# y in the side work's PSUM bank: a fixed window for C h, a third bank for A dt

## The chip, the cores and the metric

The kernel runs on one core of one Trainium2 chip. The metric is the device time of one execution in microseconds; before the change it was 2876.79 us (median of three runs, 2875.39 to 2877.91). All times below are microseconds unless marked otherwise. TensorE multiplies matrices into PSUM, which has eight banks of 512 float32 values for each of 128 partitions; VectorE (DVE), ScalarE (ACT) and GpSimd (POOL) do the elementwise work, and the sync engine's queue (SP) issues the DMAs.

## The reference, cut to what matters

The input x is 2 sequences of 1024 tokens with 512 features. The first block is a selective state space model whose state has 512 x 128 values a token; the second is a gated feed-forward net. Both are followed by a layer norm.

```python
xn = rms_norm(x) * norm_w
xn = xn * sigmoid((xn @ select_proj_w.T + select_proj_b) * select_gate)
delta, B_ssm, C_ssm = split(xn @ x_proj_w.T)            # 128 columns each
dt = softplus(delta @ dt_proj_w.T + dt_proj_b)
A = -exp(A_log)
# for every token, in order:
h = exp(dt[:, :, None] * A) * h + (dt * xt)[:, :, None] * bt[:, None, :]
y = einsum('bdn,bn->bd', h, ct)
# then
x = layernorm(x + (y + x * D_param) @ out_proj_w.T)
x = layernorm(x + (silu(x @ w_gate.T) * (x @ w_up.T)) @ w_down.T)
```

## The kernel before

**Steps, halves, groups.** The 2048 tokens are cut into 64 steps of 32 tokens (S). A step is worked in two halves of 256 features each, and a half in eight groups of 32 features; `k` counts the 1024 groups, `h` the 128 halves, and `r = k % 8` is the group's place in its half. One group's state history, 32 features by 32 tokens for all 128 state values (partitions), is one scan of 1024 elements on VectorE (L708).

**What a group does.** TensorE forms `bu`, the term (dt x) B, with two matmuls (L692) from `du`, a diagonal layout that GpSimd builds (L385), and A dt for the *next* group with two matmuls (`decay_mm`, L404) from `ddt` (L375). ScalarE takes the exponential of each A dt bank (`decay_exp`, L411) into one of three `a_sb` buffers. VectorE adds the carried state to the first token of `bu` (L705; not in the first step of a sequence) and runs the scan. The bu and a matmuls of one group use different rows of the array and run beside each other.

**PSUM.** `ps_bu` has two tiles of two banks each, `ps_a` two banks, `ps_m` one bank (the tag "m" of `misc`), `ps_y` one bank. The bank of `misc` is shared by all side work of the loop: one side group fills it, another engine evacuates it, then the next may fill it.

**C h.** y is formed from the finished state history of a half while the next half runs: `y_round(h, b)` is four matmuls of 32 columns of output partitions each (L423), for eight values of b. `ROUNDS` says in which groups of the next half these rounds are issued: three in r = 1, three in r = 4, two in r = 7. y of both halves of a step lies in one bank, and `y_out` (L430) brings it out once a step: a ScalarE copy (L436) and three GpSimd operations (L437 to L439). After four steps `post` is queued.

**Side work.** Everything else is written as generators that a `Work` object steps: `pre` (projections for the next lot of tokens: ss, sel, xp, b, z, uT, t0), `post` (transposes zT, output projection op, first layer norm), `ffn` (transpose x1T, gate and up products gu, down products d, second norm) and `silu`. A generator yields "E" for work on other engines, "P" ahead of a group of TensorE work that needs the bank, and "H" between the parts of a group. `others` steps each "E" item once in each group of the main loop; `tensor` runs one part. A side group holds the bank from its first part until `others` has issued its evacuation in a later group, so at most one side group can end, and one begin, between two calls of `others`. `PARTS` gives the parts that each r earns; unused credit is kept up to 6, and at most 4 parts are run in a group. A gate/up group has 8 parts of two matmuls, a half of a down product 8 parts of one, op 8, sel and xp 4, the transposes and z 2.

**Order.** Each engine runs its instructions in the order of issue. In a group the order of issue is: `others`; at r = 0 the half's start (y_out of the step before in a step's second half; in its first half a new `pre`, `work.finish` if the next step needs a lot that isn't ready, and `load` of the next step); the bu and a matmuls; the exponentials with L705 between them; the scan; the y rounds; the side parts; then one diagonal layout of GpSimd and at certain r the carry of the state (`carry_h`, `carry_a`). `carry_a` (L348) multiplies on GpSimd and takes an exponential on ScalarE at r = 5 of a step's first half. What is left of post and ffn when the loop ends runs after it, with six banks.

Of the kernel before, what the change touches and what calls it, by code (L numbers as in the profile page):

```python
# [9 lines left out]
FP = mybir.dt.float32  # L10
AF = mybir.ActivationFunctionType
# [6 lines left out]
TC = 256  # L18


ROUNDS = ((), (0, 1, 2), (), (), (3, 4, 5), (), (), (6, 7))
PARTS = (4, 0, 3, 3, 0, 3, 3, 0)
RMS_EPS = 1e-6
LN_EPS = 1e-5

# [9 lines left out]
def kernel(  # L35
# [83 lines left out]
    pre_pool = tc.alloc_tile_pool(name="pre", bufs=1)  # L119
    step_pool = tc.alloc_tile_pool(name="step", bufs=2)  # L120
    half_pool = tc.alloc_tile_pool(name="half", bufs=2)
    ps_y = tc.alloc_tile_pool(name="ps_y", bufs=1, space=PSUM)
    ps_m = tc.alloc_tile_pool(name="ps_m", bufs=1, space=PSUM)

    bank_pool = [tc.alloc_tile_pool(name="ps_m0", bufs=6, space=PSUM)]
# [39 lines left out]
    def pre(c):  # L165
# [31 lines left out]
        yield "E"  # L197
        for m in range(NM):
            nc.scalar.activation(xT[:, m, :], xT[:, m, :], AF.Copy, scale=col(V_NORM, m))
        yield "P"  # L200
        ps = misc(f"ss_{c}")
        for k in range(NM):
            nc.tensor.matmul(  # L203
# [9 lines left out]
        for a in (slice(0, 2), slice(2, 4)):  # L213
# [1 line left out]
                xn[:, a, :], xT[:, a, :], rms.unsqueeze(1).to_broadcast([P, 2, n]), ALU.mult  # L215
            )
            yield "E"
        yield "P"


        for m in range(NM):
            ps = misc(f"sel_{c}_{m}")
            yield from matmuls(ps, sel_w, m, xn)
            nc.scalar.activation(
                u[:, m, :], ps[:, 0:n], AF.Relu,
                bias=neg[:, 1, m : m + 1], scale=neg[:, 0, m : m + 1],
            )
            nc.scalar.activation(
                dt[:, m, :], ps[:, 0:n], AF.Abs, bias=gate_b[:, m : m + 1], scale=col(V_GATE, m)
            )  # L230
            yield "P" if m + 1 < NM else "E"
        yield from softplus(dt, u)
        nc.scalar.activation(dt, dt, AF.Exp, scale=-1.0)
        yield "E"
        for a in (slice(0, 2), slice(2, 4)):
            nc.gpsimd.tensor_tensor(xn[:, a, :], xn[:, a, :], dt[:, a, :], ALU.mult)
            yield "E"
        yield "P"


        for g, dst in ((0, low), (2, c_sb)):
            ps = misc(f"xp_{c}_{g}")
            yield from matmuls(ps, xp_w, g, xn)
            nc.scalar.copy(dst, ps[:, 0:n])
            yield "P"

        ps = misc(f"b_{c}")
        for j in range(n_j):
# [8 lines left out]
        for st in range(n_s):  # L257
# [2 lines left out]
                ub_d[t0 // S + st, :, :, 1, :].rearrange("g t n -> t g n"),  # L260
                rows.unsqueeze(1).to_broadcast([S, 4, N]),
            )
        yield "P"

        for a in range(0, NM, 2):
            ps = misc(f"z_{c}_{a}")
            for m in (a, a + 1):
                nc.tensor.matmul(  # L268
                    ps[:, ts(m - a, n)], dt_w[:, ts(m, P)], low, start=True, stop=True
                )  # L270
                yield "H" if m == a else "E"
            for m in (a, a + 1):
                z = ps[:, ts(m - a, n)]
                nc.scalar.activation(u[:, m, :], z, AF.Relu, bias=col(V_DTB, m))
                nc.scalar.activation(dt[:, m, :], z, AF.Abs, bias=col(V_DTB, m))
            yield "P" if a == 0 else "E"
        yield from softplus(dt, u)
        for a in (slice(0, 2), slice(2, 4)):
            nc.gpsimd.tensor_tensor(u[:, a, :], dt[:, a, :], xn[:, a, :], ALU.mult)
            yield "E"  # L280

        for j in range(n_j):
            yield "P"
            ps = misc(f"uT_{c}_{j}")
            for m in range(NM):
                nc.tensor.transpose(ps[:, ts(m, P)], u[:, m, ts(j, P)], ident)
                if m == 1:
                    yield "H"
            yield "E"
            t = pre_pool.tile([P, D], FP, tag="row", name=f"uT_{c}_{j}")  # L290
            nc.scalar.copy(
                t.rearrange("p (g m c) -> p m g c", g=4, m=NM),
                ps.rearrange("p (m g c) -> p m g c", m=NM, g=4),
            )
            for st in range(4):
                nc.sync.dma_start(
                    ub_d[t0 // S + 4 * j + st, :, :, 0, :].rearrange("g t q -> t g q"),
                    t[ts(st, S), :].rearrange("t (g q) -> t g q", g=4),
                )
            if c == 0:  # L300
                load(0)
                diag(0, 0)
                diag(0, 1)
        yield "P"
        ps = misc(f"t0_{c}")
        for m in range(NM):
            nc.tensor.matmul(
# [40 lines left out]
    def carry_a(st):  # L348

        if st % NSB == 0:  # L350
            return
        cd = carried[st]
        nc.gpsimd.tensor_tensor(cd, a_n, cd, ALU.mult)
        nc.scalar.activation(cd, cd, AF.Exp, scale=-1.0)

    def carry_h(st, i):

# [57 lines left out]
    def y_round(h, b):  # L415


        st, i = divmod(h, 2)
        if i == 0 and b == 0:
            ys[st] = ps_y.tile([P, 512], FP, tag="y", name=f"y_{st}")  # L420
        at = 28 + 28 * b
        for m in range(NM):
            nc.tensor.matmul(  # L423
                ys[st][ts(m, 32), ts(i, 256)], cz[st % 3][:, at : at + 32],
                hs[h][:, ts(m, 64), ts(b, 4)],
                start=(i == 0 and b == 0), stop=(i == 1 and b == 7),
                skip_group_check=True,
            )

    def y_out(st):  # L430

        tt, s = divmod(st, 4)
        if s == 0:
            yrs[tt] = post_pool.tile([P, 4, P], FP, tag="yr", name=f"yr_{tt}")
        yc = post_pool.tile([P, P, 4], FP, tag="yc", name=f"yc_{st}")
        nc.scalar.copy(yc, ys.pop(st).rearrange("p (q t) -> p q t", t=4))  # L436
        nc.gpsimd.tensor_tensor(yc, yc, pick.unsqueeze(1).to_broadcast([P, P, 4]), ALU.mult)  # L437
        nc.gpsimd.tensor_tensor(yc[:, :, 0:2], yc[:, :, 0:2], yc[:, :, 2:4], ALU.add)
        nc.gpsimd.tensor_tensor(yrs[tt][:, s, :], yc[:, :, 0], yc[:, :, 1], ALU.add)  # L439
        if s == 3:  # L440
            work.add(post(tt), front=True)

    yrs = {}
# [1 line left out]
    def post(tt):  # L445
# [4 lines left out]
        yield "E"  # L450
        nc.gpsimd.tensor_tensor(zT, zT, dq.unsqueeze(2).to_broadcast([P, NM, P]), ALU.mult)
        yield "E"
        yield "P"
        ps = misc(f"zT_{tt}")
        for s in range(4):
            nc.tensor.transpose(ps[:, ts(s, P)], yrs[tt][:, s, :], ident)
# [6 lines left out]
        )  # L463
        x1 = post_pool.tile([P, D], FP, tag="x1", name=f"x1_{tt}", bufs=4)
        nc.sync.dma_start(x1, xf[tt])
        yield "P"
        ps = misc(f"op_{tt}")
        for half in (slice(0, 256), slice(256, 512)):
            for k in range(NM):
# [20 lines left out]
    def ffn(tt, row):  # L490
# [22 lines left out]
            yield "E"  # L513
        fetch(4)
        x1T = ffn_pool.tile([P, NM, P], FP, tag="x1T", name=f"x1T_{tt}")
        yield "P"
        ps = misc(f"x1T_{tt}")
        for m in range(NM):
            nc.tensor.transpose(ps[:, ts(m, P)], row[:, ts(m, P)], ident)
# [5 lines left out]
        for what in order:  # L525
            part = int(what[1])
            if what[0] == "g":
# [2 lines left out]

                for f in range(0, NH, 2):
                    fetch(at + 4)
                    yield "P"
                    ps = misc(f"gu_{tt}_{part}_{f}")
                    for b in range(2):
                        w = pieces[at + b].rearrange("p (a k h) -> p a k h", a=2, k=NM)
# [17 lines left out]
                yield "E"  # L554
            for half in range(2):
                fetch(at + 4)
                yield "P"
# [49 lines left out]
    class Work:  # L607


        def __init__(self):  # L610
            self.gens, self.holder = [], None

        def add(self, gen, front=False):
            item = [gen, next(gen)]
# [13 lines left out]
                        self.holder = None  # L628
                    self.step(item)

        def tensor(self):

            if self.holder is not None:
                if self.holder[1] != "H":
                    return False
                self.step(self.holder)
                return True
            for item in self.gens:
                if item[1] == "P":
                    self.holder = item  # L640
                    self.step(item)
                    return True
            return False

        def finish(self, item):
            while item in self.gens:
# [13 lines left out]
    bank_pool.pop().release()  # L660
    bank_pool.append(ps_m)
    ps_bu = tc.alloc_tile_pool(name="ps_bu", bufs=2, space=PSUM)
    ps_a = tc.alloc_tile_pool(name="ps_a", bufs=2, space=PSUM)
    for b in range(2):
        decay_exp(0, b, decay_mm(0, b))

    pres, begun, credit = {}, set(), 0
    for k in range(NG):
        h, m, pair = place(k)
        st, i = divmod(h, 2)  # L670
        r = k % 8
        work.others()
        if r == 0:
            hs[h] = half_pool.tile([P, 256, S], FP, tag="h", name=f"h_{h}")

            if i == 1 and st:
                y_out(st - 1)
            if i == 0:
                c = lot_of[st]
# [31 lines left out]
            bu.rearrange("p q t -> p (q t)"),  # L711
            0.0, ALU.mult, ALU.add,
        )
        if h:
            for b in ROUNDS[r]:
                y_round(h - 1, b)
        credit = min(credit + PARTS[r], 6)
        for _ in range(min(credit, 4) if PARTS[r] else 0):
            if not work.tensor():
                break  # L720
            credit -= 1

        j, r4 = divmod(k, 4)
        if r4 == 3:
# [7 lines left out]
                carry_h(st + 1, 0)  # L732
        if r == 5 and i == 0 and st + 1 < NS:
            carry_a(st + 1)
    for j in range(8):
        y_round(2 * NS - 1, j)
    y_out(NS - 1)
    ps_a.release()
    ps_bu.release()
    bank_pool[0] = tc.alloc_tile_pool(name="ps_m2", bufs=6, space=PSUM)  # L740
# [4 lines left out]
        work.others()  # L745
        work.tensor()

    for pool in (bank_pool[0], ps_m, ps_y, hid_pool[0], ffn_pool, post_pool, main):
        pool.release()


# [65 lines left out]
```

## Time and profile before

| | |
|---|---|
| median of 3 runs | 2876.79 |
| profiled execution, its own time | 2875.05 |
| its span | 2873.2 |
| granted TensorE clock, mean | 0.985 |
| first scan starts, last scan ends | 42.5, 2785.2 |
| DVE scan L708 | 1024 x 2.287 |
| DVE carry add L705 | 992 x 0.187 |
| ACT exponential L411 | 2048 x 0.585 busy 1089.0 |
| GpSimd diagonals L375, L385 | 512 x 1.048 and 512 x 1.049 |
| ACT copy of y L436 | 64 x 0.585 |
| GpSimd L437, L438, L439 | 64 x 1.039, 0.612, 0.415 |
| ScalarE waiting for A dt (L411 on L404) | 957.1 in 710 waits |
| TensorE weight loads of a waiting for ACT | 19.9 in 68 waits |
| GpSimd ddt waiting for a's matmuls | 310.2 in 100 waits |

A float32 matmul appears as two records. Busy times of one engine are unions, so matmuls that run beside each other count once. In a row of a group the last part is the idle time of the engine just before such instructions and what ended most of it. In rows in order of time the first number is the start from the span's beginning, the second the length, and a bracket gives idle time before the row and what ended it.

### The profile page before, as it was taken

The numbers are of one execution on the slowest core, as the hardware profiler recorded it, in microseconds if no ns is written. First come the engines' busy times: TensorE is split into PE (matmuls) and PEld (weight loads), VectorE is DVE, ScalarE is ACT, GpSimd is POOL, SyncE is SP. The second block draws the span as 40 slices with busy tenths as digits, with TensorE's granted clock in tenths as the row PEclk, the third lists the DMA queues.
The fourth block names the chain that finished last, engine by engine and source line by source line (L and its number), as shares of the span: only waits on it lengthen the run. The fifth ranks groups of instructions, "written<-read, shape, count | busy, mean of one in ns | idle before, by whom it ended". The sixth has DMA issues, their size and how long they took to land.

```text
span 2873.2 us, 57382 instructions
## 1 busy us (share of the span) xinstructions
PE 2751.4 (96%) x22728; PEld 1496.3 (52%) x22728; DVE 2532.2 (88%) x2176; ACT 1561.8 (54%) x3105; POOL 1783.0 (62%) x2016
## 2 busy tenths in 40 slices
PE   7879899999999999999999999999999999999998
PEld 4324455555555555455555555555555555555558
DVE  3999799899998999999999999999999999999970
ACT  4545555555565556645555555555556555555543
POOL 4556665666666666666567667566665666666643
PEclk6999999999999999999999999999999999999999
DMA  2011221324213231222312233122321322333236
GB/s 74 16 30 65 78 87 61 105 66 133 85 53 112 89 107 62 82 98 89 111 51 88 97 103 109 56 84 92 114 96 51 115 96 91 114 101 100 98 112 230
DMA packets 112379, 258.66 MB, mean 90 GB/s; under 512 B 11568, under 2 KB 49456, under 8 KB 112112
## 3 DMA queue, kind: packets, MB, share of 16 engines
q1 hardware_dynamic: 112112, 254.99, 27.4%
q8 instruction: 181, 2.97, 0.4%
q14 instruction: 86, 0.70, 0.1%
HBM read 242.23 MB, written 12.71 MB: 89 GB/s over the span
## 4 chain that ended last, share of the span: by engine, by line
PE 75%; DVE 18%; issue 3%; ACT 2%; POOL 1%; DMA 0%; SPq 0%; DVEq 0%; POOLq 0%; ACTq 0%
PE bu L692 27%; PE gu L539 17%; DVE h L708 16%; PE y L423 13%; PE d L561 6%; PE a L404 5%; PE sel L186 2%; PE op L470 1%; PE xp L186 1%; DVE bu L705 1%; ACT a_sb L411 1%; PE b L250 1%; PE ss L203 0%; PE z L268 0%; DMA ub_d<-uT 0%
## 5 line engine op out<-in xcount | busy, mean ns | idle before, releaser
L708 DVE TENSOR_TENSOR_SCAN h<-a_sb,bu 128x1024 f32<-128x1024 f32 x1024 | 2341.2, 2287 | 160.7 <-PE bu L692 46.3
L411 ACT ACTIVATE a_sb<-a 128x496 f32<-128x496 f32 x2048 | 1089.0, 585 | 1078.5 <-PE a L404 957.1
L404 PE MATMUL a<-ddt,a_t 32*128 32x512 f32 x4096 | 1253.9, 647 | 3.0 <-ACT t L314 2.8
L692 PE MATMUL bu<-du,ub 32*128 32x512 f32 x4096 | 1210.5, 647 | 47.9 <-DVE h L708 27.3
L375 POOL TENSOR_TENSOR ddt<-dt,hot 128x512 f32<-128x512 f32 x512 | 532.6, 1048 | 310.2 <-PE a L404 310.2
L539 PEld LDWEIGHTS gu<-x1T,w 128*128 128x128 f32 x4096 | 482.2, 192 | 230.9 <-issue 181.3
L385 POOL TENSOR_TENSOR du<-ub,hot 128x512 f32<-128x512 f32 x512 | 535.0, 1049 | 48.9 <-PE a L404 44.9
L539 PE MATMUL gu<-x1T,w 128*128 128x128 f32 x4096 | 537.1, 283 | 11.7 <-DVE x L474 4.0
L692 PEld LDWEIGHTS bu<-du,ub 32*128 32x128 f32 x4096 | 342.9, 185 | 376.9 <-issue 206.8
L423 PE MATMUL y<-h,cz 128*32 128x256 f32 x8192 | 527.3, 386 | 1.3 <-DVE h L708 1.3
L423 PEld LDWEIGHTS y<-h,cz 128*32 128x32 f32 x8192 | 228.2, 110 | 407.8 <-issue 296.4
L404 PEld LDWEIGHTS a<-ddt,a_t 32*128 32x128 f32 x4096 | 379.4, 185 | 31.3 <-ACT a_sb L411 19.9
L579 POOL TENSOR_SCALAR gu<-gu 128x256 f32<-128x256 f32 x128 | 108.3, 846 | 309.6 <-ACT gu L547 309.3
L705 DVE TENSOR_TENSOR bu<-bu,cd 128x32 f32<-128x32 f32 x992 | 185.6, 187 | 98.2 <-PE a L404 92.0
L561 PE MATMUL d<-w,hid 128*128 128x256 f32 x1024 | 256.7, 393 | 12.6 <-ACT t L314 4.4
L561 PEld LDWEIGHTS d<-w,hid 128*128 128x128 f32 x1024 | 183.9, 190 | 131.7 <-issue 86.1
L437 POOL TENSOR_TENSOR yc<-yc,pick 128x512 f32<-128x512 f32 x64 | 66.5, 1039 | 151.1 <-ACT yc L436 151.0
L362 POOL TENSOR_TENSOR cd<-cd,h 128x256 f32<-128x256 f32 x124 | 106.4, 858 | 45.5 <-DVE h L708 45.5
L587 POOL TENSOR_TENSOR hid<-gu,e 128x256 f32<-128x256 f32 x128 | 93.0, 727 | 62.1 <-ACT e L585 60.2
L547 ACT COPY gu<-gu 128x512 f32<-128x512 f32 x128 | 75.1, 587 | 63.2 <-PE gu L539 63.1
L580 POOL TENSOR_TENSOR gu<-gu 128x256 f32<-128x256 f32 x128 | 94.2, 736 | 10.7
L567 DVE TENSOR_TENSOR x<-x,d 128x256 f32<-128x256 f32 x64 | 25.6, 399 | 72.3 <-PE d L561 72.3
(86 smaller groups left out, 1272.1 us busy)
## 6 DMA issues: line engine op xcount, KB each, us to landing
w<-in_wgu_s_dram SPq DMA_DIRECT2D x256, 512.0 KB, 3.6
w<-in_wd_s_dram SPq DMA_DIRECT2D x128, 512.0 KB, 3.6
cd<-dt_d SPq DMA_DIRECT2D x62, 256.0 KB, 3.9
ub<-ub_d SPq DMA_DIRECT2D x64, 128.0 KB, 2.0
ub_d<-bt SPq DMA_DIRECT2D x64, 64.0 KB, 1.8
ub_d<-uT SPq DMA_DIRECT2D x64, 64.0 KB, 1.8
zT<-in_x_q_dram SPq DMA_DIRECT2D x16, 256.0 KB, 4.1
x<-in_x_dram SPq DMA_DIRECT2D x16, 256.0 KB, 3.8
```

Of the source, the lines that this page charges most:

```text
L362: nc.gpsimd.tensor_tensor(cd, cd, last, ALU.mult)
L375: nc.gpsimd.tensor_tensor(ddts[j][:, m, :, :], made[lot_of[st]][0][:, a + m, toks(st)].unsqueeze(1).to_broadcast([P, 16, S]), hot[:, ts(i, ...
L385: nc.gpsimd.tensor_tensor(dus[j][:, m, :, :], uv[:, a + m, :].unsqueeze(2).to_broadcast([P, 16, S]), hot.unsqueeze(1).to_broadcast([P, 16, ...
L404: nc.tensor.matmul(ps, a_t[ts(g, 32), m, :], ddts[k // 4][ts(g, 32), m % 2, :, :], start=True, stop=True,)
L411: nc.scalar.activation(a_sb[:, k % 3, ts(b, 16), 1:], ps[:, :, 1:], AF.Exp, scale=-1.0)
L423: nc.tensor.matmul(ys[st][ts(m, 32), ts(i, 256)], cz[st % 3][:, at : at + 32], hs[h][:, ts(m, 64), ts(b, 4)], start=(i == 0 and b == 0), s ...
L539: nc.tensor.matmul(ps[:, ts(2 * a + b, P)], w[:, a, k, :], x1T[:, k, :], start=(k == 0), stop=(k == NM - 1),)
L561: nc.tensor.matmul(ps[:, 0:HD], hid[:, f, :], w[:, f % 4, :], start=(f == 0), stop=(f == NH - 1),)
L579: nc.gpsimd.tensor_scalar_max(g, g, -80.0)
L692: nc.tensor.matmul(bu[:, ts(b, 16), :], prepared[st][ts(g, 32), 1, :], dus[k // 4][ts(g, 32), m % 2, :, :], start=True, stop=True,)
L705: nc.vector.tensor_tensor(first, first, left[:, at : at + 2, i, :], ALU.add)
L708: nc.vector.tensor_tensor_scan(hs[h][:, ts(r, 32), :].rearrange("p q t -> p (q t)"), a_sb[:, k % 3, :, :].rearrange("p q t -> p (q t)"), b ...
```

## The change

y of each half (no longer of each step) goes into the one bank of `misc`, and `ps_y` is gone; `ps_a` has three banks. The y rounds of the finished half are issued in r = 1, 2 and 3 (three, three and two), and `y_out` is called at r = 4 for a half, with tiles of half the width. Side parts run only in r = 0, 4, 5, 6 and 7, up to four in each. Where a generator yielded "P" it now yields the number of parts of the group ahead; `tensor` starts a group only if that number fits the room left until the y rounds (`ROOM`, less the parts already run). Ahead of the first y round `idle` runs out a group that still holds the bank. Parts no longer earn credit. `carry_exp`, the exponential of `carry_a`, is issued at r = 7 instead of r = 5.

```diff
-ROUNDS = ((), (0, 1, 2), (), (), (3, 4, 5), (), (), (6, 7))
-PARTS = (4, 0, 3, 3, 0, 3, 3, 0)
+ROUNDS = ((), (0, 1, 2), (3, 4, 5), (6, 7), (), (), (), ())
+PARTS = (4, 0, 0, 0, 4, 4, 4, 4)
+
+ROOM = (4, 0, 0, 0, 20, 16, 12, 8)
...
-    ps_y = tc.alloc_tile_pool(name="ps_y", bufs=1, space=PSUM)
...
-        yield "P"
+        yield NM
...
-                    yield "P"
+                    yield 2 * NM
...
-        nc.scalar.activation(cd, cd, AF.Exp, scale=-1.0)
+
+    def carry_exp(st):
+        if st % NSB:
+            nc.scalar.activation(carried[st], carried[st], AF.Exp, scale=-1.0)
...
-        st, i = divmod(h, 2)
-        if i == 0 and b == 0:
-            ys[st] = ps_y.tile([P, 512], FP, tag="y", name=f"y_{st}")
+        if b == 0:
+            ys[h] = misc(f"y_{h}")
...
-                ys[st][ts(m, 32), ts(i, 256)], cz[st % 3][:, at : at + 32],
+                ys[h][ts(m, 32), 0:256], cz[h // 2 % 3][:, at : at + 32],
                 hs[h][:, ts(m, 64), ts(b, 4)],
-                start=(i == 0 and b == 0), stop=(i == 1 and b == 7),
+                start=(b == 0), stop=(b == 7),
...
-        yc = post_pool.tile([P, P, 4], FP, tag="yc", name=f"yc_{st}")
-        nc.scalar.copy(yc, ys.pop(st).rearrange("p (q t) -> p q t", t=4))
-        nc.gpsimd.tensor_tensor(yc, yc, pick.unsqueeze(1).to_broadcast([P, P, 4]), ALU.mult)
+        yc = post_pool.tile([P, 64, 4], FP, tag="yc", name=f"yc_{h}", bufs=2)
+        nc.scalar.copy(yc, ys.pop(h)[:, 0:256].rearrange("p (q t) -> p q t", t=4))
+        nc.gpsimd.tensor_tensor(yc, yc, pick.unsqueeze(1).to_broadcast([P, 64, 4]), ALU.mult)
         nc.gpsimd.tensor_tensor(yc[:, :, 0:2], yc[:, :, 0:2], yc[:, :, 2:4], ALU.add)
-        nc.gpsimd.tensor_tensor(yrs[tt][:, s, :], yc[:, :, 0], yc[:, :, 1], ALU.add)
-        if s == 3:
+        nc.gpsimd.tensor_tensor(yrs[tt][:, s, ts(i, 64)], yc[:, :, 0], yc[:, :, 1], ALU.add)
+        if s == 3 and i == 1:
             work.add(post(tt), front=True)
...
-        def tensor(self):
+        def tensor(self, room=64):
...
+                self.left -= 1
                 self.step(self.holder)
                 return True
             for item in self.gens:
-                if item[1] == "P":
-                    self.holder = item
+                if item[1] != "E" and item[1] <= room:
+                    self.holder, self.left = item, item[1] - 1
                     self.step(item)
                     return True
             return False
 
+        def idle(self):
+
+            while self.holder is not None:
+                self.others()
+                if self.holder is not None:
+                    self.tensor()
+
...
-    ps_a = tc.alloc_tile_pool(name="ps_a", bufs=2, space=PSUM)
+    ps_a = tc.alloc_tile_pool(name="ps_a", bufs=3, space=PSUM)
...
         work.others()
+        if r == 4 and h:
+            y_out(h - 1)
         if r == 0:
             hs[h] = half_pool.tile([P, 256, S], FP, tag="h", name=f"h_{h}")
-
-            if i == 1 and st:
-                y_out(st - 1)
...
-        if h:
+        if ROUNDS[r] and h:
+            if r == 1:
+                work.idle()
             for b in ROUNDS[r]:
                 y_round(h - 1, b)
-        credit = min(credit + PARTS[r], 6)
-        for _ in range(min(credit, 4) if PARTS[r] else 0):
-            if not work.tensor():
-                break
-            credit -= 1
+        done = 0
+        while done < PARTS[r] and work.tensor(ROOM[r] - done):
+            done += 1
...
+        if r == 7 and i == 0 and st + 1 < NS:
+            carry_exp(st + 1)
+    work.idle()
     for j in range(8):
         y_round(2 * NS - 1, j)
-    y_out(NS - 1)
+    y_out(2 * NS - 1)
```

More of the change, by code (lines that the diff above doesn't have):

```diff
@@ L217, in pre @@
             yield "E"
-        yield "P"
+        yield NM
         for m in range(NM):
@@ L230, in pre @@
             )
-            yield "P" if m + 1 < NM else "E"
+            yield NM if m + 1 < NM else "E"
         yield from softplus(dt, u)
@@ L237, in pre @@
             yield "E"
-        yield "P"
+        yield NM
         for g, dst in ((0, low), (2, c_sb)):
@@ L244, in pre @@
             nc.scalar.copy(dst, ps[:, 0:n])
-            yield "P"
+            yield NM if g == 0 else n_j
         ps = misc(f"b_{c}")
@@ L262, in pre @@
             )
-        yield "P"
+        yield 2
         for a in range(0, NM, 2):
@@ L275, in pre @@
                 nc.scalar.activation(dt[:, m, :], z, AF.Abs, bias=col(V_DTB, m))
-            yield "P" if a == 0 else "E"
+            yield 2 if a == 0 else "E"
         yield from softplus(dt, u)
@@ L282, in pre @@
         for j in range(n_j):
-            yield "P"
+            yield 2
             ps = misc(f"uT_{c}_{j}")
@@ L303, in pre @@
                 diag(0, 1)
-        yield "P"
+        yield 1
         ps = misc(f"t0_{c}")
@@ L423, in y_round, with y_out @@
             nc.tensor.matmul(
-                ys[st][ts(m, 32), ts(i, 256)], cz[st % 3][:, at : at + 32],
+                ys[h][ts(m, 32), 0:256], cz[h // 2 % 3][:, at : at + 32],
                 hs[h][:, ts(m, 64), ts(b, 4)],
-                start=(i == 0 and b == 0), stop=(i == 1 and b == 7),
+                start=(b == 0), stop=(b == 7),
                 skip_group_check=True,
             )
-    def y_out(st):
+    def y_out(h):
+        st, i = divmod(h, 2)
         tt, s = divmod(st, 4)
-        if s == 0:
+        if s == 0 and i == 0:
             yrs[tt] = post_pool.tile([P, 4, P], FP, tag="yr", name=f"yr_{tt}")
-        yc = post_pool.tile([P, P, 4], FP, tag="yc", name=f"yc_{st}")
-        nc.scalar.copy(yc, ys.pop(st).rearrange("p (q t) -> p q t", t=4))
-        nc.gpsimd.tensor_tensor(yc, yc, pick.unsqueeze(1).to_broadcast([P, P, 4]), ALU.mult)
+        yc = post_pool.tile([P, 64, 4], FP, tag="yc", name=f"yc_{h}", bufs=2)
+        nc.scalar.copy(yc, ys.pop(h)[:, 0:256].rearrange("p (q t) -> p q t", t=4))
+        nc.gpsimd.tensor_tensor(yc, yc, pick.unsqueeze(1).to_broadcast([P, 64, 4]), ALU.mult)
         nc.gpsimd.tensor_tensor(yc[:, :, 0:2], yc[:, :, 0:2], yc[:, :, 2:4], ALU.add)
-        nc.gpsimd.tensor_tensor(yrs[tt][:, s, :], yc[:, :, 0], yc[:, :, 1], ALU.add)
-        if s == 3:
+        nc.gpsimd.tensor_tensor(yrs[tt][:, s, ts(i, 64)], yc[:, :, 0], yc[:, :, 1], ALU.add)
+        if s == 3 and i == 1:
             work.add(post(tt), front=True)
@@ L452, in post @@
         yield "E"
-        yield "P"
+        yield 2
         ps = misc(f"zT_{tt}")
@@ L465, in post @@
         nc.sync.dma_start(x1, xf[tt])
-        yield "P"
+        yield 2 * NM
         ps = misc(f"op_{tt}")
@@ L515, in ffn @@
         x1T = ffn_pool.tile([P, NM, P], FP, tag="x1T", name=f"x1T_{tt}")
-        yield "P"
+        yield 2
         ps = misc(f"x1T_{tt}")
@@ L532, in ffn @@
                     fetch(at + 4)
-                    yield "P"
+                    yield 2 * NM
                     ps = misc(f"gu_{tt}_{part}_{f}")
@@ L556, in ffn @@
                 fetch(at + 4)
-                yield "P"
+                yield NH
                 ps = misc(f"d_{tt}_{part}_{half}")
@@ L610, in __init__ @@
         def __init__(self):
-            self.gens, self.holder = [], None
+            self.gens, self.holder, self.left = [], None, 0
         def add(self, gen, front=False):
@@ L662 @@
     ps_bu = tc.alloc_tile_pool(name="ps_bu", bufs=2, space=PSUM)
-    ps_a = tc.alloc_tile_pool(name="ps_a", bufs=2, space=PSUM)
+    ps_a = tc.alloc_tile_pool(name="ps_a", bufs=3, space=PSUM)
     for b in range(2):
         decay_exp(0, b, decay_mm(0, b))
-    pres, begun, credit = {}, set(), 0
+    pres, begun = {}, set()
     for k in range(NG):
@@ L746 @@
         work.tensor()
-    for pool in (bank_pool[0], ps_m, ps_y, hid_pool[0], ffn_pool, post_pool, main):
+    for pool in (bank_pool[0], ps_m, hid_pool[0], ffn_pool, post_pool, main):
         pool.release()
```

## The prediction

> **What bounds the kernel now.** I read the page's busy rows and chain first, then the groups, then the rows in time.
>
> ```profile
> span 2873.2 us, 57382 instructions
> PE 2751.4 (96%) x22728; PEld 1496.3 (52%) x22728; DVE 2532.2 (88%) x2176; ACT 1561.8 (54%) x3105; POOL 1783.0 (62%) x2016
> PE 75%; DVE 18%; issue 3%; ACT 2%; POOL 1%; DMA 0%; SPq 0%; DVEq 0%; POOLq 0%; ACTq 0%
> L708 DVE TENSOR_TENSOR_SCAN h<-a_sb,bu 128x1024 f32<-128x1024 f32 x1024 | 2341.2, 2287 | 160.7 <-PE bu L692 46.3
> L404 PE MATMUL a<-ddt,a_t 32*128 32x512 f32 x4096 | 1253.9, 647 | 3.0 <-ACT t L314 2.8
> ```
>
> Two engines carry the chain: TensorE most of it, VectorE nearly a fifth. So the order of the work inside a half matters, not only its sum. The windows split at the last scan's end show the loop and what is left after it (columns: length, busy time and instructions by engine):
>
> ```profile
> 42.50:2785.20 2742.70, 2652.22 (x22055) 1407.93 (x22052) 2525.26 (x2161) 1516.95 (x3008) 1730.31 (x1927) 0.99 0.27 86
> 2785.20:2873.20 88.00, 77.65 (x578) 71.44 (x578) 6.96 (x15) 28.03 (x59) 31.40 (x43) 0.97 0.62 207
> ```
>
> The TensorE rows of one half (start, length), mid-loop:
>
> ```profile
> 1406.37 0.69 PE L692 MATMUL bu<-du,ub 32*128 32x512 f32 x1
> ...
> 1407.44 2.05 PE L539 MATMUL gu<-x1T,w 128*128 128x128 f32 x16
> 1409.42 0.69 PE L692 MATMUL bu<-du,ub 32*128 32x512 f32 x1
> ...
> 1410.49 1.50 PE L423 MATMUL y<-h,cz 128*32 128x256 f32 x24
> 1411.93 0.69 PE L692 MATMUL bu<-du,ub 32*128 32x512 f32 x1
> ...
> 1419.67 0.69 PE L692 MATMUL bu<-du,ub 32*128 32x512 f32 x1
> 1419.91 0.69 PE L404 MATMUL a<-ddt,a_t 32*128 32x512 f32 x1
> ```
>
> and of VectorE:
>
> ```profile
> 1405.44 2.29 DVE L708 TENSOR_TENSOR_SCAN h<-a_sb,bu 128x1024 f32<-128x1024 f32 x1
> 1407.65 0.18 DVE L705 TENSOR_TENSOR bu<-bu,cd 128x32 f32<-128x32 f32 x1
> 1407.93 2.29 DVE L708 TENSOR_TENSOR_SCAN h<-a_sb,bu 128x1024 f32<-128x1024 f32 x1
> 1410.67 0.20 DVE L705 TENSOR_TENSOR bu<-bu,cd 128x32 f32<-128x32 f32 x1 [0.45 <-PE a L404]
> 1410.97 2.29 DVE L708 TENSOR_TENSOR_SCAN h<-a_sb,bu 128x1024 f32<-128x1024 f32 x1
> ```
>
> From these rows come all units. A group on TensorE is its bu and a (1.07: 1406.37 to 1407.44) and what follows: four gate/up parts 1.98 (to 1409.42), three y rounds 1.44 (1410.49 to 1411.93), two y rounds 1.00, four parts of sel, op or d 1.92. One gate/up part alone takes 0.64 where four take 1.98, so each chunk has a fixed 0.2. A fed scan follows the last by 2.48 (1405.44 to 1407.93); one that waits for TensorE starts 1.55 after its bu (1409.42 to 1410.97). bu has two buffers: a group's bu starts at the earliest some 0.18 after the scan two groups back.
>
> VectorE's floor of the loop is 992 groups at 2.48 and 32 at 2.20 (the steps that begin a sequence have no carry): 2534. The loop takes 2742.7, so 209 are lost. Eight groups at 2.48 are 19.9 a half; the shown one takes 21.14 (bu at 1398.52 and at 1419.66).
>
> **The change, part by part.**
>
> *y moved to the half's groups 1, 2, 3.* Before, the groups held 4, y3, 3, 3, y3, 3, 3, y2: about 2.1 to 3.05 on TensorE, mixed around the scan's 2.48. After, they hold (up to 4), y3, y3, y2, 4, 4, 4, 4: three groups near the scan (2.51, 2.51, 2.07), then four of 3.05 together. Walk one half, with bu at time B and scan at S, starting at group 4 with VectorE fed (S 2.5 after B):
>
> group 4: B 0, S 2.50; 5: 3.05, 4.98; 6: 6.11, 7.66; 7: 9.16, 10.71; 0: 12.21, 13.76; 1: 13.28, 16.24; 2: 16.3, 18.7; 3: 18.8, 21.2; next 4: 21.18, S 23.68.
>
> Only 0.95 of VectorE backlog (2.50 less 1.55) covers the four long groups' excess of 4 x 0.57 = 2.28, so 1.3 is lost every half that has 16 gate/up parts: 21.2, no better than the 21.14 shown. In groups 0 to 3 TensorE is early and can't use it: the side groups of 8 parts don't fit group 0's room of 4.
>
> *Which halves occur.* I followed the yields with the diff's constants, group by group (a side group ends at the next "others", a new one starts only with room). The same count on the old constants gives the old trace's 3712 gate/up and 912 down records in the loop. After: 57 of the 127 whole halves have groups 4 to 7 loaded and group 0 empty; 48 have group 0 loaded as well (sel, x1T, zT, z, uT); 12 have two loaded groups; 10 are other light ones. Times: the first kind 21.2. The light kinds lose a few tenths: 20.1 and 20.6. The second kind is TensorE-bound: 8 x 1.07 + 3.88 + 4 x 1.95 = 20.2, plus 0.6 to 1.9 in group 0, plus 0.3 to 1.8 of waits for the shared bank (below): 22.3 to 23.6, taken at 22.6, near the light ones, x1T and uT being more frequent than sel. Sum: 57 x 21.2 + 48 x 22.6 + 12 x 20.1 + 10 x 20.6 = 2740, the half left over 20, and about 4 for the slower clock at the start (the page's clock row begins at 6; the first half took 23.9): **2764, +22 on 2742.7**.
>
> This sum holds three gains, not to be added again. Chunks fall from 588 to 515, 73 x 0.2 = 14 of TensorE. The forced finish of the preparation in the step before 352 us (one scan waited 10.7) is no longer needed by the count. The third bank is the next point.
>
> *Third A dt bank.* With two, the second a of a group waits for the exponential of the group before: in the rows above the last a starts at 1419.91 instead of 1419.68, 0.23 late, after a short y group; side work in group 0 starts late by 23 in all, in group 1 by 9. The third bank removes the first kind. But after an empty group 0 (1.07 long) the exponentials of 1.06 for the pair are still running, so group 1's second a stays late by 0.5; TensorE is early there, so it costs nothing. Below: the whole 32 gained; above: none, where the scans run at 2.48 through it, as they do here (1405.44 and 1407.93 follow such groups). Taken inside the walk.
>
> *One bank for y and side work.* The first y in group 1 now waits for the last side group's evacuation, and the first side group in group 4 for the y copy. **A rule against it**: the Trainium skill, "PSUM — Partial Sum Buffer", in its summary of rules for kernel authors, says to target a different bank when PSUM is read while matmuls run. Taken as exposed each time, the copies of 0.37 and 0.59 would cost 127 x 0.96 = 122. The row says otherwise for ScalarE: a 512-wide copy takes 0.587 (gu, L547) and the next group's bu and a cover it with 1.07: zero. It says yes for VectorE: zT's add of 0.66 queues behind a scan, and op after zT began 2.57 after its bu instead of 1.07 (1457.63 against 1455.06), 1.5 lost. I take the rows; these are the 0.3 to 1.8 above. If the 1.07 cover failed it would be the 122.
>
> *y_out per half.* ScalarE: two copies of 256, by the 0.37 of bt (L256), for one of 0.585: +0.16 a step, 10 in all, on an engine idle 46%. GpSimd: the nearest rows for the halved sizes are 0.73, 0.42 and about 0.3, twice, against 2.07: +0.8 a step, 53 in all. It is hidden: ddt waits 310 for TensorE to release its buffer. Uncovered, it would delay ddt and so a, by at most 0.8 a step. The zT chain starts from y_out as before.
>
> *carry_exp two groups later.* It no longer holds ScalarE's exponentials behind GpSimd's carry (15.3 in 16 waits); its reader comes two groups after it. Nothing to at most 15 gained; I take nothing, ScalarE having slack. DMA: weights are fetched four pieces ahead as before and no TensorE wait on them shows; SP's order is the same.
>
> *The rest after the loop.* 320 gate/up and 96 down records are left for 384 and 112: 64 x 0.115 + 16 x 0.215 = 10.8 less, about 2 of which a barer chain of norm and silu gives back: **-9**.
>
> Sum: 2873.2 + 22 - 9 = 2886 for the profiled run's span, +13. Its own time is 2875.05, the runs' median 2876.79, so the forecast is **2890**.
>
> **Rivals.** *A, the forecast*, 2890 (2883 to 2905).
> *B, bank and fewer chunks win*, faster. If the long stretch costs 0.6 instead of 1.3 (VectorE further behind when it starts), the 57 halves give 57 x 0.6 = 34: +13 - 34, so 2856. For it: 209 of slack, and the a waits. Against: the two bu buffers, which bound the backlog at 0.95.
> *C, the shared bank decides*: VectorE's evacuations cost 0.6 more in the 48 loaded halves, 29: 2919. For it: zT to op above. Against: most evacuations are ScalarE's.
> *D, it cancels*, within 0.2% (5.8 us, about what a measurement of this kernel can tell from no change): +13 is a small difference of two large sums; 2877.
> That no third bank comes into being is out: y's pool gave up exactly one of eight.
>
> Chances: A 0.52, B 0.20, C 0.13, D 0.15. Slower by over 0.2%: A and C, 0.65; faster: B. The range takes in half of B and most of C: 2862 to 2916; A's own range stands above.
>
> **What would show it.** Right: in steady halves the scans run at 2.48 in groups 0 to 3 and at 3.05 in groups 6 and 7; VectorE idles before L705 more than 98, by over 30; a's wait in group 0 is gone; y in group 1 starts 1.07 after bu, later where x1T, sel or zT came before; the tail is near 79. Wrong: full halves under 20.8 (B), or y or the first side group of group 4 regularly waiting for ScalarE's copy (C), or a forced finish still there.

## The result, and the profile after

| | before | after |
|---|---|---|
| median (4 runs each) | 2876.09 (2873.32 to 2877.91) | 2892.0 (2890.58 to 2894.73) |
| profiled execution, its own time | 2875.05 | 2892.83 |
| its span | 2873.2 | 2890.9 |
| first scan to last scan end | 2742.7 | 2772.7 |
| after the last scan | 88.0 | 75.8 |

The change makes the kernel slower: the ratio after to before is 1.0057, with a 95% interval of 1.004 to 1.0075. The loop became 30.0 longer and the rest after it 12.2 shorter. The page of the kernel after, its busy rows, its chain and the groups that answer to those of before:

```profile
span 2890.9 us, 58034 instructions
PE 2718.5 (94%) x22728; PEld 1449.1 (50%) x22728; DVE 2535.9 (88%) x2176; ACT 1570.7 (54%) x3169; POOL 1816.6 (63%) x2208
PE 67%; DVE 22%; issue 4%; POOL 4%; ACT 3%; DMA 0%; SPq 0%; DVEq 0%; ACTq 0%; POOLq 0%
L720 DVE TENSOR_TENSOR_SCAN h<-a_sb,bu 128x1024 f32<-128x1024 f32 x1024 | 2340.5, 2287 | 154.4 <-PE bu L704 42.4
L408 PE MATMUL a<-ddt,a_t 32*128 32x512 f32 x4096 | 1244.0, 653 | 2.8 <-ACT t L315 2.8
L717 DVE TENSOR_TENSOR bu<-bu,cd 128x32 f32<-128x32 f32 x992 | 184.7, 186 | 130.3 <-PE a L408 125.8
```

TensorE is busy 33 less (2751.4 before, 2718.5 now), with the same 22728 records, in a span that is 18 longer. So it wasn't the amount of its work that grew. VectorE idles 130.3 ahead of the carry add, where the row of before has 98.2:

```profile
L705 DVE TENSOR_TENSOR bu<-bu,cd 128x32 f32<-128x32 f32 x992 | 185.6, 187 | 98.2 <-PE a L404 92.0
```

It also makes up more of the chain (22%, before 18%). The windows split at the last scan's end, with the same columns as before:

```profile
42.40:2815.10 2772.70, 2631.63 (x22131) 1371.76 (x22126) 2529.34 (x2162) 1528.72 (x3077) 1768.42 (x2123) 0.98 0.27 86
2815.10:2890.90 75.80, 65.44 (x504) 59.90 (x504) 6.53 (x14) 25.21 (x54) 28.34 (x40) 0.99 0.61 205
```

The first row carries the loss: 20.6 less of TensorE work takes 30.0 more time. The VectorE rows of one full half (start, length, idle before the row in the bracket) show where it goes:

```profile
1736.82 2.29 DVE L720 TENSOR_TENSOR_SCAN h<-a_sb,bu 128x1024 f32<-128x1024 f32 x1
...
1739.30 2.29 DVE L720 TENSOR_TENSOR_SCAN h<-a_sb,bu 128x1024 f32<-128x1024 f32 x1
...
1741.94 2.29 DVE L720 TENSOR_TENSOR_SCAN h<-a_sb,bu 128x1024 f32<-128x1024 f32 x1
1744.69 0.20 DVE L717 TENSOR_TENSOR bu<-bu,cd 128x32 f32<-128x32 f32 x1 [0.46 <-PE a L408]
1744.99 2.29 DVE L720 TENSOR_TENSOR_SCAN h<-a_sb,bu 128x1024 f32<-128x1024 f32 x1
1747.81 0.20 DVE L717 TENSOR_TENSOR bu<-bu,cd 128x32 f32<-128x32 f32 x1 [0.53 <-PE a L408]
1748.11 2.29 DVE L720 TENSOR_TENSOR_SCAN h<-a_sb,bu 128x1024 f32<-128x1024 f32 x1
...
1750.59 2.29 DVE L720 TENSOR_TENSOR_SCAN h<-a_sb,bu 128x1024 f32<-128x1024 f32 x1
```

These are the scans of groups 4, 5, 6, 7, 0 and 1. Scan to scan they are 2.48, 2.64, 3.05, 3.12 and 2.48 apart: group 6 is late by 0.16, group 7 by 0.57 and group 0 by 0.64, 1.37 in the half. TensorE can't work ahead of the long stretch, since bu has two buffers: its row at the start of the same group 4 waits for VectorE (the bracket).

```profile
1734.29 0.66 PE L704 MATMUL bu<-du,ub 32*128 32x512 f32 x1 [0.22 <-DVE bu L717]
```

Whether this is a loss against the old order, halves of equal work tell. Those whose only side work is sixteen gate/up parts, timed from the scan of a group 4 to that of the next, take 20.9 on average in the kernel before (20 of them) and 21.3 in the kernel after (30). That is 12 of the loop's 30; other halves of equal work are too few in the two kernels to compare.

### The profile page after: what moved, and what is told of

Same layout as the page of the kernel before. It is cut to its first block, busy times and chain, and to the rows that moved or that the text cites. A ratio compares the mean times of both kernels' runs of the same rounds, so it can differ in the third digit from the quotient of the medians.

```text
span 2890.9 us, 58034 instructions
## 1 busy us (share of the span) xinstructions
PE 2718.5 (94%) x22728; PEld 1449.1 (50%) x22728; DVE 2535.9 (88%) x2176; ACT 1570.7 (54%) x3169; POOL 1816.6 (63%) x2208
## 4 chain that ended last, share of the span: by engine, by line
PE 67%; DVE 22%; issue 4%; POOL 4%; ACT 3%; DMA 0%; SPq 0%; DVEq 0%; ACTq 0%; POOLq 0%
PE bu L704 24%; DVE h L720 20%; PE gu L543 17%; PE y L426 11%; PE d L565 6%; PE a L408 4%; PE sel L187 2%; DVE bu L717 1%; PE xp L187 1%; ACT a_sb L415 1%; POOL ddt L379 1%; POOL xT L215 1%; POOL du L389 1%; PE b L251 1%; ACT dt L276 0%
## 5 line engine op out<-in xcount | busy, mean ns | idle before, releaser
L704 PE MATMUL bu<-du,ub 32*128 32x512 f32 x4096 | 1180.2, 650 | 77.3 <-DVE bu L717 66.0
L543 PEld LDWEIGHTS gu<-x1T,w 128*128 128x128 f32 x4096 | 475.4, 192 | 191.0 <-issue 96.7
L704 PEld LDWEIGHTS bu<-du,ub 32*128 32x128 f32 x4096 | 330.7, 186 | 449.9 <-issue 293.8
L426 PE MATMUL y<-h,cz 128*32 128x256 f32 x8192 | 534.2, 391 | 19.8 <-DVE zT L465 11.0
L543 PE MATMUL gu<-x1T,w 128*128 128x128 f32 x4096 | 520.6, 281 | 10.3 <-ACT t L315 4.2
L408 PEld LDWEIGHTS a<-ddt,a_t 32*128 32x128 f32 x4096 | 347.9, 186 | 44.5 <-ACT a_sb L415 40.2
L717 DVE TENSOR_TENSOR bu<-bu,cd 128x32 f32<-128x32 f32 x992 | 184.7, 186 | 130.3 <-PE a L408 125.8
L441 POOL TENSOR_TENSOR yc<-yc,pick 128x256 f32<-128x256 f32 x128 | 78.4, 612 | 273.1 <-ACT yc L440 273.1
L187 PE MATMUL sel<-xT,sel_w 128*128 128x256 f32 (+1 forms) x288 | 71.1, 399 | 16.6 <-POOL ddt L379 6.5
```

The costliest lines, as they stand in the source:

```text
L187: nc.tensor.matmul(ps[:, 0:n], w[:, k, ts(m, P)], rhs[:, k, :], start=(k == 0), stop=(k == NM - 1),)
L408: nc.tensor.matmul(ps, a_t[ts(g, 32), m, :], ddts[k // 4][ts(g, 32), m % 2, :, :], start=True, stop=True,)
L426: nc.tensor.matmul(ys[h][ts(m, 32), 0:256], cz[h // 2 % 3][:, at : at + 32], hs[h][:, ts(m, 64), ts(b, 4)], start=(b == 0), stop=(b == 7), ...
L543: nc.tensor.matmul(ps[:, ts(2 * a + b, P)], w[:, a, k, :], x1T[:, k, :], start=(k == 0), stop=(k == NM - 1),)
L704: nc.tensor.matmul(bu[:, ts(b, 16), :], prepared[st][ts(g, 32), 1, :], dus[k // 4][ts(g, 32), m % 2, :, :], start=True, stop=True,)
L717: nc.vector.tensor_tensor(first, first, left[:, at : at + 2, i, :], ALU.add)
```

## The experiments

Each kernel was timed against the kernel before on the same chip in the same session; ratios are to it, with 95% intervals.

**Two banks for A dt** (the kernel after, without the third bank):

```diff
-    ps_a = tc.alloc_tile_pool(name="ps_a", bufs=3, space=PSUM)
+    ps_a = tc.alloc_tile_pool(name="ps_a", bufs=2, space=PSUM)
```

> The changed kernel with two A dt banks instead of three (one PSUM bank stays unused). Theory (the third bank repays part of the packing): after the empty group 0 and the short y group both a matmuls of the next group wait for the exponentials; summed over the loop the side work's late starts grow from about 50 to 140 us, about 35 of which reach the path: 2927 us, ratio to before 1.018. Rival (the waits lie under the scans, the third bank is worth nothing): 2892 us, 1.006.

Measured: 2933.74 (2933.16 to 2940.9), ratio 1.0213 (1.0195 to 1.0232). Its loop is 38.0 longer than the loop after.

**y in a bank of its own** (the kernel after, with two banks for A dt and y taken out of the shared bank):

```diff
+    ps_y = tc.alloc_tile_pool(name="ps_y", bufs=1, space=PSUM)
...
-            ys[h] = misc(f"y_{h}")
+            ys[h] = ps_y.tile([P, 512], FP, tag="y", name=f"y_{h}")
...
-    ps_a = tc.alloc_tile_pool(name="ps_a", bufs=3, space=PSUM)
+    ps_a = tc.alloc_tile_pool(name="ps_a", bufs=2, space=PSUM)
```

> As the two-bank kernel, but y gets a bank of its own again (its tiles stay one per half, its place in groups 1 to 3 too), so nothing is shared between y and the side work: the PSUM layout is that of before, only the order is packed. Theory (packing the side work into groups 4 to 7 and 0 is what costs): still clearly slower than before, about 2912 us, 1.0125, and only some 15 us under the two-bank kernel. Rival (the shared bank is what costs): at the level of before, 2876 us, and 40 or more under the two-bank kernel.

Measured: 2915.23 (2911.93 to 2923.48), ratio 1.0148 (1.0127 to 1.0168). The weight loads of A dt show the wait that the third bank removes. First the two-bank kernel's row, then that of the kernel after (the last part is idle time and what ended it):

```profile
L408 PEld LDWEIGHTS a<-ddt,a_t 32*128 32x128 f32 x4096 | 387.8, 186 | 75.5 <-ACT a_sb L415 59.8 <-POOL gu L583 8.7 <-issue 3.8
```

```profile
L408 PEld LDWEIGHTS a<-ddt,a_t 32*128 32x128 f32 x4096 | 347.9, 186 | 44.5 <-ACT a_sb L415 40.2 <-issue 3.7
```

The wait for ScalarE's exponential falls from 59.8 to 40.2. What is left lies mostly in group 1 after an empty group 0: where a later experiment fills that group, the wait is 4.2. Since the two-bank kernel and the kernel after differ in the banks of A dt alone, the third bank is worth 1.0213 - 1.0057, about 1.6%, or 45; by the medians, 2933.7 - 2892.0, it is 42. In the kernel before, this wait was only 19.9, and with the new order and y in its own bank it is 59.5: most of what the bank gains is a wait that the new order had made. The expected gain of 35 came about, but not by the expected rise of the side work's late starts from 50 to 140: in the rows those rise from 53 to 73 only, and y in group 1 is late by 120 where it was 82.

The price of sharing is 2933.7 - 2915.2 = 18.5, with two banks for A dt in both kernels; with three it can't be measured, as that would take nine banks.

**y and its output a half at a time, in the old order** (the kernel before with its own y bank, `ROUNDS` and `PARTS`, and y and `y_out` for every half):

```diff
-            ys[st] = ps_y.tile([P, 512], FP, tag="y", name=f"y_{st}")
+            ys[h] = ps_y.tile([P, 512], FP, tag="y", name=f"y_{h}")
...
-            if i == 1 and st:
-                y_out(st - 1)
+            if h > 1:
+                y_out(h - 2)
```

> The kernel before with y formed and brought out per half, as in the changed kernel (tiles of half the width, y_out once a half, here at group 0), but in a bank of its own and with the old rounds, parts and two A dt banks. Theory (y_out per half is covered, as priced at nothing; the cost lies in the packed order): at the level of before, within 5 us of 2875. Rival (the additional copies and GpSimd operations are part of the loss): 10 to 20 us slower, so that the own-bank packed kernel's 39 us is only half due to the order.

Measured: 2874.89 (2871.29 to 2879.65, 12 runs), ratio 1.0009 (0.9999 to 1.0018). The doubled copies and GpSimd operations cost nothing that shows. The change then splits into four terms, in ratios: y a half at a time 0.1%; the order of the groups (from here to y in its own bank, with whole side groups only, the earlier `y_out` and the moved exponential of the carry) +1.4%; the shared bank +0.65%; the third bank -1.6%. The terms belong to this sequence of steps: the 1.4% holds waits for A dt that the third bank then takes away.

**Filling idle TensorE time** (the kernel after, with two matmuls whose products nobody reads, in groups that may run side parts and have none, when the bank is free):

```diff
+        if PARTS[r] and not done and work.holder is None and 16 < k < NG - 16:
+            ps = misc(f"fill_{k}")
+            for b in range(2):
+                nc.tensor.matmul(
+                    ps[:, ts(b, 256)], ident, a_t.rearrange("p m n -> p (m n)")[:, 0:256],
+                    start=True, stop=True,
+                )
```

> The changed kernel with two unread 128x256 matmuls in each group that may run side parts but has none. Theory (in light halves TensorE idles so much that its granted clock falls to half for 3.4 to 6.8 us, which the y rounds behind them pay): about 8 us faster than the changed kernel, 2884 us, 1.003, with no half-clock stretch after 230 us. Rival (only the long stretch of loaded groups counts): 2892 us or, as the filler takes TensorE time, a little more.

Measured: 2887.43 (2884.39 to 2887.77), ratio 1.0044 (1.0029 to 1.0059): 4.6 below the kernel after, with ranges that don't overlap though the intervals of the ratios do. The windows tell why. The first row is a light half of the kernel after (side work in groups 4 and 5 only), the second a full one (the third column from the end is the granted clock):

```profile
616.00:628.00 12.00, 10.07 (x72) 3.36 (x72) 9.90 (x10) 6.18 (x13) 8.28 (x10) 0.72 0.15 45
640.00:652.00 12.00, 11.50 (x109) 5.28 (x112) 10.88 (x12) 6.28 (x13) 4.71 (x6) 1.00 0.31 104
```

and the groups of the first row in the kernel with the filler, which reaches them 8.2 earlier:

```profile
607.84:619.84 12.00, 12.00 (x112) 5.28 (x112) 11.15 (x10) 7.18 (x15) 9.08 (x10) 1.00 0.14 45
```

With work that serves nothing, the clock stays at 1.00 where it had been 0.72, and VectorE is busy 11.15 of 12.00 where it was 9.90. The loop is 5.9 shorter. That is a net figure, since the filler also runs in the empty group 0 of full halves: half by half, the 14 halves that met half clock in the kernel after are 17.4 shorter with the filler, and the other 112 are 11.7 longer. So half clock costs the kernel after more than the 5.9; an estimate from these halves is 17. The expected "no half-clock stretch after 230 us" did not come: four of 3.4 are left in the loop.

**Long groups apart** (the kernel before, parts and y rounds spread evenly):

```diff
-ROUNDS = ((), (0, 1, 2), (), (), (3, 4, 5), (), (), (6, 7))
-PARTS = (4, 0, 3, 3, 0, 3, 3, 0)
+ROUNDS = ((), (0, 1), (2,), (3,), (4,), (5,), (6,), (7,))
+PARTS = (3, 1, 2, 2, 2, 2, 2, 2)
```

> The kernel before with its y rounds and side parts spread evenly: two rounds in group 1, one in each of 2 to 7, and 3, 1, 2, 2, 2, 2, 2, 2 parts. Banks and parts per half as before. Theory (what matters is how far a group's TensorE time leaves the scan's 2.48 us): every group is near 2.4, waits for exponentials and banks fall by a third, about 2805 us, ratio 0.975. Rival (each chunk's fixed 0.14 to 0.2 us counts): seven y chunks for three and eight side chunks for five in a half are about 1 us more, 128 us in all less what hides: slower, above 2900 us.

Measured: 2966.99 (2960.94 to 2970.13), ratio 1.0316 (1.0296 to 1.0337). The theory failed and the rival held. TensorE's rows of one group (start, length) show the term it had left out:

```profile
1399.38 0.69 PE L692 MATMUL bu<-du,ub 32*128 32x512 f32 x1
...
1400.45 0.64 PE L423 MATMUL y<-h,cz 128*32 128x256 f32 x8
1401.02 1.16 PE L539 MATMUL gu<-x1T,w 128*128 128x128 f32 x8
1402.11 0.69 PE L692 MATMUL bu<-du,ub 32*128 32x512 f32 x1
```

bu and a 1.07, one y round 0.57, two parts 1.09: 2.73, where every group should have stayed near the scan's 2.48. One y round costs 0.57, not a third of 1.44, and the two parts 1.09, not half of 1.98. Each piece of another kind that TensorE begins in a group costs some 0.1 to 0.2 beside its matmuls. From the second step on there are 905 pieces of side work in this loop, 584 before, and four more pieces of y in each half. As an estimate from these costs, 321 x 0.19 and 127 x 4 x 0.13 make 127; the loop is 111 longer.

**y in two groups** (the kernel after with four rounds each in groups 1 and 2, and the freed group 3 given to side parts):

```diff
-ROUNDS = ((), (0, 1, 2), (3, 4, 5), (6, 7), (), (), (), ())
-PARTS = (4, 0, 0, 0, 4, 4, 4, 4)
+ROUNDS = ((), (0, 1, 2, 3), (4, 5, 6, 7), (), (), (), (), ())
+PARTS = (4, 0, 0, 3, 3, 2, 4, 4)
-ROOM = (4, 0, 0, 0, 20, 16, 12, 8)
+ROOM = (4, 0, 0, 20, 17, 14, 12, 8)
...
-        if r == 4 and h:
+        if r == 3 and h:
```

> The changed kernel (shared bank, three A dt banks) with the y rounds four and four in groups 1 and 2, y_out at group 3, and parts 4, 0, 0, 3, 3, 2, 4, 4, so that the loaded stretch has five groups, three of them near 2.5 us and two of 3.05. Theory (the loss comes from the excess of the loaded stretch over the two-buffer backlog): the excess of 4 x 0.57 falls to 2 x 0.57 plus two y groups of 2.94 just before: about 14 us faster than the changed kernel, 2878 us, 1.001. Rival (the loss is the shared bank's waits and the clock): no change, 2892 us, 1.006.

Measured: 2888.37 (2888.26 to 2893.12), ratio 1.0047 (1.0034 to 1.0061): too near the kernel after to tell. In the profiled execution, the slowest of the five, the loop is 8.1 longer than after, and the rest 7.5 shorter. Halves with sixteen gate/up parts and nothing else do take 21.0 on average (35 of them), for 21.3 in the kernel after, so the other halves lose more than these gain. There are 646 pieces of side work from the second step on for 510. The two effects can't be told apart in this run.

**Other parts in the old order.** Four more kernels change only `ROUNDS` and `PARTS` of the kernel before. The first:

```diff
-ROUNDS = ((), (0, 1, 2), (), (), (3, 4, 5), (), (), (6, 7))
-PARTS = (4, 0, 3, 3, 0, 3, 3, 0)
+ROUNDS = ((), (0, 1, 2), (), (), (3, 4), (), (), (5, 6, 7))
+PARTS = (2, 0, 4, 2, 0, 4, 4, 0)
```

> The kernel before with y rounds 3, 2, 3 in groups 1, 4, 7 (was 3, 3, 2) and parts 2, 0, 4, 2, 0, 4, 4, 0 (was 4, 0, 3, 3, 0, 3, 3, 0), so that a gate/up group runs as two chunks of four and the short y group stands where a's wait is shorter. Theory (chunks' fixed 0.2 us and a's waits after short groups are what the old order loses, beside the groups' spread round 2.48): about 17 us faster than before, 2859 us, 0.994. Rival (the old order is bound by the sums on TensorE and VectorE, which stay): 2876 us, 1.000.

Measured: 2849.0 (2846.64 to 2849.48), ratio 0.9907 (0.9894 to 0.9921). It is faster than both kernels. The second keeps the old rounds and takes the new parts alone:

```diff
-PARTS = (4, 0, 3, 3, 0, 3, 3, 0)
+PARTS = (2, 0, 4, 2, 0, 4, 4, 0)
```

> The kernel before with only the parts changed, to 2, 0, 4, 2, 0, 4, 4, 0; y rounds 3, 3, 2 as before. It splits the gain of the 3, 2, 3 kernel (2849 us). Theory (chunks of four parts save the fixed cost of a third chunk): most of the gain is here, about 2855 us, 0.993. Rival (the y round moved to group 7, which shortens a's wait in group 0, made it): 2870 us or more, 0.998.

Measured: 2846.71 (2845.33 to 2850.96), ratio 0.9911 (0.9894 to 0.9927). So the parts alone bring the gain. The reason that the theory gave, fewer pieces, fails: from the second step on there are 581 for 584. The last two split the parts; in the text below, "the fourth kernel's parts" are these, (2, 0, 4, 2, 0, 4, 4, 0).

```diff
-PARTS = (4, 0, 3, 3, 0, 3, 3, 0)
+PARTS = (2, 0, 3, 3, 0, 4, 4, 0)
```

> The kernel before with PARTS (2, 0, 3, 3, 0, 4, 4, 0): group 0 earns 2 parts in place of 4, groups 5 and 6 take the two up, groups 2 and 3 stay at 3 and 3. Theory (the gain of the fourth kernel's parts lies in group 0: its four parts follow the two y rounds of group 7, and their start was late by 23 in all behind the exponential of the bank of A dt that group 7's short stretch had not yet freed): most of the gain of 28 stays, about 2853, 0.993, and the late starts in group 0 fall from 23 to under 8. Rival (the gain lies in filling 4 and 2 in place of 3 and 3): nearly none of it, 2868 or more.

Measured: 2881.57 (2873.29 to 2883.84, 20 runs), ratio 1.0025 (1.0017 to 1.0033): a little slower than before. The late starts in group 0 did not fall from 23 to under 8; they are 28.

```diff
-PARTS = (4, 0, 3, 3, 0, 3, 3, 0)
+PARTS = (4, 0, 4, 2, 0, 4, 2, 0)
```

> The kernel before with PARTS (4, 0, 4, 2, 0, 4, 2, 0): group 0 keeps its 4 parts, each pair of groups between y rounds gets 4 and 2 in place of 3 and 3. Theory (the gain lies in group 0): no more than 6 below the kernel before, about 2870, 0.999. Rival (the gain lies in 4 and 2, since the scan after a y group is fed late and a long group first is covered by nothing, or the reverse: the order of long and short decides): about 2855, 0.994.

Measured: 2857.24 (2856.6 to 2857.79), ratio 0.9933 (0.9915 to 0.9951). The theory of group 0 fell: two parts there, with 3 and 3 left, lose 0.25%, and 4 and 2 gain most of it with group 0 as it was. Split at the last scan's end, against the profiled execution of before:

| parts | loop | after the loop | gate/up and down records left for it |
|---|---|---|---|
| 4 0 3 3 0 3 3 0 (before) | 2742.7 | 88.0 | 384, 112 |
| 2 0 3 3 0 4 4 0 | -6.0 | +12.2 | 448, 128 |
| 4 0 4 2 0 4 2 0 | -11.6 | -7.3 | 328, 96 |
| 2 0 4 2 0 4 4 0 | -18.4 | -12.2 | 320, 96 |

Two things are at work. Some 12 of the 30 by which the last one's profiled span is shorter lie after the loop: the parts decide how much work is left when it ends. In the page of the last of the table, the chain and VectorE's wait speak for the rest:

```profile
PE 73%; DVE 20%; issue 3%; ACT 2%; POOL 1%; DMA 0%; SPq 0%; DVEq 0%; POOLq 0%; ACTq 0%
...
L705 DVE TENSOR_TENSOR bu<-bu,cd 128x32 f32<-128x32 f32 x992 | 183.6, 185 | 84.8 <-PE a L404 77.0
```

TensorE is 73% of the chain for 75% before, and VectorE's idle time before the carry add falls from 98.2 to 84.8, the reverse of what the change did. The number of side pieces hardly moves; their sizes do. In the rows of before, 40 groups hold one gate/up part and 70 hold three, since a side group of eight parts ends inside a group and the next can't begin there. The last of the table has 2 and 2 such groups, 98 with two parts and 185 with four. That four and two beat three and one is shown by the times. The reason isn't: in both orders no more than two groups with side work follow each other, so the backlog of 0.95 in the prediction doesn't tell them apart, and no run isolates another cause.

## Why the prediction was right

The likeliest case, 2890 with its own range of 2883 to 2905, is what came: 2892.0. The mechanism, a long stretch that outruns VectorE's backlog, is in the rows. That the number is off by 2 only is luck in part, since two errors of 16 and 17 cancelled. Its steps one by one:

- **The walk of a full half: right, shown in the rows.** 30 halves with sixteen gate/up parts and an empty group 0 take 21.3 on average; the walk gave 21.2. The scans fall behind at the places it names, by 1.37 for 1.3. The 21.14 that it was held against was a long half of the kernel before: its average is 20.9, so the new order loses 0.4 in such a half. What was too neat is "2.48 in groups 0 to 3": group 0's own scan is the latest of all, since it follows group 7's long stretch.
- **Counts of halves: right; sizes: right in sum only, with three errors.** The rows hold the same 57, 48 and 12 halves. The second kind, taken at 22.6, measured 22.25 on average. The first kind, with all its contents, is 21.49 for 21.2. The third, taken at 20.1, is 20.0 to 20.6 in five halves with full clock and 20.6 to 22.3 in seven that met half clock, 20.9 on average. The first two errors, -17 and +16, cancel, by luck: 22.6 came from a span of 22.3 to 23.6 that doesn't follow from its terms (20.2 with 0.6 to 1.9 and 0.3 to 1.8 is 21.1 to 23.9). The light halves of the third kind add about 10 over the forecast. The loop came to +30.0 for +22.
- **The term that was mis-sized: the light halves.** The prediction let them lose "a few tenths" and took TensorE's durations as fixed. They are not, when TensorE idles: see below.
- **Third bank inside the walk: right in direction, the bound from above was too low.** The prediction bounded it by the 32 of late starts in the kernel before. In the new order it was worth 42 to 45. Nothing in the forecast's time hung on it, because the walk had no such wait in it. After an empty group 0, y in group 1 starts 0.85 late and not 0.5, and TensorE is early there, as said.
- **The shared bank: right.** Its whole price is 18.5. The rule that the prediction names against it, taken as exposed each time, would have made 122; the row of ScalarE's copy behind the next 1.07 of bu and a was the better guide. Weight loads of gate/up do wait for y's copy regularly (45 times, 34.1 in all), but under that 1.07: work in group 4 starts late by 6 in all. Where group 0 was loaded, y starts late by 23 in all, half of it behind zT (1.7 to 1.8 in each of seven halves), whose evacuation queues behind a scan; behind sel and x1T it is about 0.1 or less. Rival C asked for 29 above the forecast and did not come.
- **`y_out` for each half at nothing: right**, by the run in the old order (0.1%). GpSimd's busy time grew by 33.6 (1783.0 to 1816.6), not by 53. It shows in 4% of the chain (before 1%), but with ddt, xT and du (1% each) and not with y's output, although that waits for the copy of y:

```profile
L441 POOL TENSOR_TENSOR yc<-yc,pick 128x256 f32<-128x256 f32 x128 | 78.4, 612 | 273.1 <-ACT yc L440 273.1
```

Twice as many operations wait, 273.1 in all for 151.0 before. Why GpSimd's share of the chain grew stays open.
- **Fewer pieces: counted rightly in number (515 in the loop), but with no proof of their worth.** The even kernel shows that more pieces cost time.
- **The rest after the loop: -12.2 for -9.** The records left are the 320 and 96 of the count. TensorE's gate/up time there fell by 8.5 and its down time by 3.7, so that all 12.2 arrived; the 2 that a barer chain was to give back were not there.
- **Carry's exponential two groups later** was taken at nothing and was not tried alone; it lies inside the +1.4% of the order. ScalarE's wait of 15.3 for the carry is gone in the kernel after.

One sum of a rival is off: if the long stretch cost 0.6 instead of 1.3, the gain would be 57 x 0.7 = 40 and not 34, so B stood at 2850. It did not come either way.

Not tried: a third buffer for bu, which would raise the backlog that bounds the long stretch (six banks for bu, none left), and three banks for A dt with a bank for y (nine in all). So the bound itself is shown by the rows alone, and no run takes it away.

## What to carry to other kernels

When two engines hand over group by group, with two buffers between them, a longer stretch of one is free only as far as the other's backlog reaches (here 0.95 of an excess of 2.28); lay the groups out along that backlog before counting how much work is saved. A bank that is won for one wait is to be priced in the order it will serve: here it paid for a wait of the new order rather than for one of the old. And change the sizes of the pieces first: one line of constants gained 0.9% where the new order lost 0.6%.

## What the runs showed of the hardware

**The clock dropped with no gap longer than about one microsecond before it.** In the light half at 616 the clock is granted at 0.72 over 12.00, and y's rounds of group 1 stretch. TensorE's rows of the kernel after (start, length), from the half-clock stretch to the next y group:

```profile
622.55 1.06 PE L704 MATMUL bu<-du,ub 32*128 32x512 f32 x1
...
623.58 2.79 PE L426 MATMUL y<-h,cz 128*32 128x256 f32 x24
...
627.44 1.50 PE L426 MATMUL y<-h,cz 128*32 128x256 f32 x24
```

The same 24 records take 2.79 and 1.50. The Trainium skill, "TensorE: Matmul & The Clock Gate", in "Why this matters for your kernels", warns of gaps over some 3 us between bursts. Here no gap is so long: from 606 to the fall at 619.7 the only idle time of TensorE over 0.3 is one of 1.02, at 618.1, where it waited for VectorE's carry add. The half clock then lasted until 626.5. From 213 us to the last scan the clock falls nine times, and a gap of 1.02 to 1.87 begins in the 2.2 us before each fall. But such a gap doesn't decide it: 30 others of 0.94 to 1.58 in the same stretch are followed by no fall for 8 us, this one for instance, with the clock at 1.00 from 574 to 590:

```profile
580.64 1.50 PE L426 MATMUL y<-h,cz 128*32 128x256 f32 x24 [1.58 <-DVE zT L465]
```

So gaps under 3 us put the clock at risk here, and what decides between them these traces don't show. In that stretch half clock adds up to 47.8 in the kernel after, 23.9 in the one before, and 13.6 with the filler.

**Each piece that begins has a price.** One gate/up part takes 0.64, two 1.09, four 1.98, and one y round 0.57 where three take 1.44: about 0.45 a part or round, and 0.1 to 0.2 for the start.
